# First expert layer: every token through every expert, or kept experts' tokens placed in 160 rows each

## The chip, the cores and the metric

The kernel runs on one core of one Trainium2 chip. The metric is the device time of one execution in microseconds (us). Three executions of the kernel before took 3815.05, 3818.07 and 3828.3 us; the median is 3818.07 us. Differences below about 0.3% (11.5 us) can't be told from no change here.

## What is computed

The program is a chain of layers over x, 16 sequences of 64 tokens with 256 features: T = 1024 tokens, held as 8 tiles of 128 tokens. Before the part that changes stands a linear-attention encoder of four layers (`l0_attn`), after it a slot attention over a context of 1601 rows for each sequence (`l1_xattn`). The part itself is a mixture of experts; x is layer-normed on the way in and the result is added to x:

```
logits = x @ gate_w.T;  probs = softmax(logits)
top2_w, top2_idx = top_k(probs, 2)
cap = int(1.25 * T / E)                       # 160 for T = 1024, E = 8
counts = bincount(top2_idx.reshape(-1), length=E);  keep = counts <= cap
comb[t, e] = top2_w where e is one of t's two experts, times keep[e]
h = relu(einsum('th,ehf->tef', x, W1) + b1);  y = einsum('teh,ehf->tef', h, W2) + b2
out = einsum('te,tef->tf', comb, y)
```

So an expert chosen more than 160 times gives nothing at all, and a kept expert has at most 160 tokens.

## The kernel before

Everything is in float32. A product in float32 shows as two records on the matrix engine (PE), so "x16" of a product is 8 of them.

**`l0_attn` (L408 to L735)** runs the encoder in two halves of 512 tokens, `a` and `b`. Its order is written by hand: generators (`project`, `attend`, `feed`) yield after each piece of PE work and `go(it, n)` (L650) advances one of them n pieces. While `self.pinned` is set, the engines keep the order of the program for PE (`mm`, `tr`), VectorE (`V`), ScalarE (`A`) and GpSimd (`G`). The last calls are `go(fd)` (rest of `feed(a)`), `go(feed(b, w, True))` and `squares(999)` (L732 to L734). `feed` (L613) turns the normed tokens, evacuates one half on VectorE and one on ScalarE (`turn`, L461), makes 8 products of 512 columns for the hidden layer (`by_feature`), then 4 tiles of tokens from them (`by_token`), norms the result and, in the last layer, adds it to x (`finish`, L642).

Between these pieces ScalarE squares the context for the next stage: `context_squares` (L242) has 16 x 13 = 208 squares of 128x256, loaded three pieces ahead; `squares(n)` advances it by n. A `feed` asks for 1 or 2 after each hidden product and for 4, 4, 4, 2 after the tiles of tokens, 26 in all.

**`l0_ffn` (L752 to L794)** norms all of x (`layernorm`), turns it (`transpose`) into xT, makes the logits tile by tile (`lin`), then on VectorE and ScalarE softmax, ranks and selection, counts each expert's tokens by a product with ones (L775), and makes `comb`. The experts' second bias is added as comb times b2 (L785). Then `weighted_experts` (L737) takes the 8 experts one after the other: 8 products of 512 columns into hT (`lin_t`, L180), relu alternating between VectorE and ScalarE (`bias_relu`), 16 products of 256 columns (`lin`, L193), and for every tile x += comb[:, e] * product (L746). All 1024 tokens go through all experts. PE, VectorE and ScalarE are ordered here by the framework's scheduler.

Each expert's two weights (256 KB each) go into a ring of 8 buffers (`w2`, L103), so four experts' weights are there at most. SyncE (SP) issues the loads in the order that the scheduler gives it; an issue that waits holds those behind it.

**`l1_xattn` (L796)** begins with two context loads for the first slot tile (`load_keys`, `cT`, 1664 KB each), whose buffers lie over memory that `l0_ffn` used, so that they wait for the tile they overlap (here xT, last read by `lin_t`). Its first scores need x of the first tile and both `cT`.

Of the kernel before, what the change touches and what calls it, by code (L numbers as in the profile page):

```python
# [11 lines left out]
F32 = mybir.dt.float32  # L12
I32 = mybir.dt.int32
# [50 lines left out]
class Sections:  # L64
# [343 lines left out]
    def l0_attn(self):  # L408
        nc, tc, d = self.nc, self.tc, self.d
        HT = NT // 2  # L410
        with ExitStack() as ctx:
# [260 lines left out]

            less = sb.tile([P, 1], F32, tag="minus", name="minus")
# [59 lines left out]
            go(feed(b, w, True))  # L733
            squares(999)  # L734
            self.pinned = False  # L735
# [16 lines left out]
    def l0_ffn(self):  # L752
        nc, tc, d = self.nc, self.tc, self.d
        E = 8
        with ExitStack() as ctx:
            sb = ctx.enter_context(tc.tile_pool(name="l0f", bufs=1, reuse_waits="tile"))
            sb2 = ctx.enter_context(tc.tile_pool(name="l0f2", bufs=2, reuse_waits="tile"))
            ps = ctx.enter_context(tc.tile_pool(name="l0f_ps", bufs=2, space=PSUM, reuse_waits="tile"))
            wg = sb.tile([P, KC, E], F32, tag="wg", name="wg")
            nc.sync.dma_start(wg, d["L0_ffn_gate_w"].rearrange("(c p) n -> p c n", p=P))  # L760
            b2 = sb.tile([E, D], F32, tag="b2", name="b2")
            nc.sync.dma_start(b2, d["L0_ffn_b2"])
            xln = sb.tile([P, NT, D], F32, tag="xln", name="xln")
            xT = sb.tile([P, KC, T], F32, tag="xT", name="xT")
            self.layernorm(sb, self.x, xln)
            self.transpose(ps, xln, xT)
            probs = sb.tile([P, NT, E], F32, tag="probs", name="probs")
            self.lin(ps, wg, xT, lambda t, pm: self.copy(probs[:, t, :], pm))
            self.softmax_small(sb, probs, E)
            sel = self.ranks(sb, probs, E)  # L770
            nc.vector.tensor_scalar(sel, sel, 1.5, None, ALU.is_lt)
            cnt = sb.tile([P, E], F32, tag="cnt", name="cnt")
            nc.vector.tensor_reduce(cnt, sel.rearrange("p t e -> p e t"), AX.X, ALU.add)
            pc = ps.tile([P, E], F32, tag="mm", name="pc", padded_shape=[P, 512])
            nc.tensor.matmul(pc, self.c("ones"), cnt, start=True, stop=True)  # L775
            keep = sb.tile([P, E], F32, tag="keep", name="keep")
            cap = int(1.25 * T / E)
            nc.vector.tensor_scalar(keep, pc, float(cap), None, ALU.is_le)
            comb = sb.tile([P, NT, E], F32, tag="comb", name="comb")
            nc.vector.tensor_tensor(comb, probs, sel, ALU.mult)  # L780
# [1667 lines left out]
def _consts():  # L2448
# [20 lines left out]
        "odd": (np.arange(P)[:, None] % 2 == np.arange(2)[None, :]).astype(np.float32),  # L2469
    }  # L2470


def _buckets():

    rp = np.maximum(np.arange(S)[:, None] - np.arange(S)[None, :], 0)
# [109 lines left out]
```

## Time and profile before

| what | value |
| --- | --- |
| median of three runs | 3818.07 us |
| the profiled execution | 3822.79 us |
| its span | 3821.0 us |
| granted PE clock, mean | 0.964 |
| PE, VectorE, ScalarE, GpSimd busy | 92%, 52%, 38%, 33% of the span |
| last `feed` and `l0_ffn` | about 1286 to 1464 us of the span |

The profiled execution is one of its own, 1.8 us longer than its span and 4.7 us longer than the median. The profile is read in four ways here: the chain of work that ended last (start, duration, engine, tile, line, number of records), a table of busy time by stretches (busy us and number of instructions for each engine, granted PE clock, share of DMA time, GB/s), the instructions of one engine in order of time (start, duration, line, operation; in brackets how long the engine was idle before and what released it), and the list of DMA queues. Lines of the pinned helpers show as L2233 (products), L2238 (transposes) and L58 (VectorE, ScalarE, GpSimd in `l0_attn`).

### The profile page before, as it was taken

To read this page: it belongs to the slowest core of one execution; us is meant where nothing else is said; L and a number is where in the kernel's file an instruction comes from. 1 tells how busy PE (TensorE), PEld (TensorE's weight loads), DVE (VectorE), ACT (ScalarE), POOL (GpSimd) and SP (SyncE) were. 2 spreads that over 40 slices of the span, in tenths; PEclk is the share of its full clock that TensorE was granted. 3 is DMA by queue.
4 is the path that set the end of the run, shared out by engine and by line. 5 is a ranking of instruction groups with operands and counts; after the bars stand their busy time and mean duration, and the time that the engine had idled before them with its cause. 6 is when DMAs were issued, how large, how long until landed. Compare 5 with 4: busy or idle time off the path is not lost.

```text
span 3821.0 us, 71159 instructions
## 1 busy us (share of the span) xinstructions
PE 3522.3 (92%) x31163; PEld 2225.8 (58%) x31178; DVE 1991.1 (52%) x3664; ACT 1457.4 (38%) x2080; POOL 1260.9 (33%) x755
## 2 busy tenths in 40 slices
PE   8999999996999899999987898999999879999986
PEld 4555555563666555555545566676767655555454
DVE  4333333335555546566556644577776655333346
ACT  3333333333444302444433433366666612111214
POOL 1555555551110002334331100477777630000012
PEclk9999999998999899999989999999999979999997
DMA  3111110001333214422301000311111004111650
GB/s 124 37 37 37 37 37 22 35 27 46 100 98 95 78 31 171 144 99 81 108 25 40 1 6 0 110 37 55 38 55 37 8 4 168 36 42 32 249 201 13
DMA packets 99678, 248.86 MB, mean 65 GB/s; under 512 B 8180, under 2 KB 69247, under 8 KB 97192
## 3 DMA queue, kind: packets, MB, share of 16 engines
q1 hardware_dynamic: 92456, 217.05, 16.0%
q10 hardware_dynamic: 6912, 27.27, 2.3%
q8 instruction: 245, 4.01, 0.4%
q14 instruction: 65, 0.53, 0.0%
HBM read 243.24 MB, written 1.05 MB: 64 GB/s over the span
## 4 chain that ended last, share of the span: by engine, by line
PE 77%; DVE 12%; ACT 8%; issue 2%; POOL 1%; DMA 0%; ACTq 0%; DVEq 0%; SPq 0%; POOLq 0%
PE sc L2233 15%; PE pk L2233 14%; PE lin L2233 7%; PE acc L2233 6%; PE lin_t L2233 5%; PE lin L193 5%; ACT e L321 4%; PE pu L2233 4%; PE gate L1798 3%; PE up L1798 3%; PE pc L1420 3%; PE prz L2233 2%; PE lin_t L180 2%; PE gelu_t L1330 2%; PE turn L2238 2%
## 5 line engine op out<-in xcount | busy, mean ns | idle before, releaser
L2166 POOL TENSOR_TENSOR tot<-tot,e 128x1024 f32<-128x1024 f32 (+1 forms) x340 | 803.5, 2363 | 373.8 <-ACT e L321 250.9
L264 DVE TENSOR_REDUCE m<-sc 128x4 f32<-128x2048 f32 x96 | 220.1, 2293 | 270.6 <-PE sc L2233 269.6
L1560 DVE SCALAR_TENSOR_TENSOR e<-sc,row_L_xattn_nbias,free 128x2048 f32<-128x2048 f32 x104 | 244.3, 2349 | 122.2 <-PE sc L2233 118.3
L1562 ACT ACTIVATE e<-e 128x2048 f32<-128x2048 f32 x104 | 198.7, 1911 | 243.2 <-DVE e L1560 243.2
L321 ACT ACTIVATE e<-sc 128x2048 f32<-128x2048 f32 x104 | 195.2, 1877 | 241.1 <-PE sc L2233 231.9
L2233 PE MATMUL sc<-qb,kT 32*128 32x128 f32 x6656 | 245.0, 283 | 36.5 <-DVE m L278 12.3
L2233 PEld LDWEIGHTS sc<-qb,kT 32*128 32x128 f32 x6656 | 206.1, 187 | 80.6 <-issue 24.5
L2233 PE MATMUL acc<-e,v 128*32 128x128 f32 x6656 | 226.3, 276 | 6.4 <-ACT e L1563 6.4
L2233 PEld LDWEIGHTS acc<-e,v 128*32 128x32 f32 x6656 | 170.0, 110 | 105.8 <-issue 95.2
L2233 PE MATMUL pk<-cT,wk 128*128 128x512 f32 (+1 forms) x512 | 206.4, 532 | 3.6 <-DVE rows L294 3.6
L2233 PE MATMUL pk<-wv,cT 128*128 128x256 f32 x832 | 208.6, 392 | 0.0
L1563 ACT ACTIVATE e<-e 128x2048 f32<-128x2048 f32 x104 | 198.7, 1911 | 3.3
L2233 PE MATMUL pk<-cT,wkv 128*128 128x512 f32 (+1 forms) x512 | 196.4, 524 | 0.0
L965 POOL TENSOR_TENSOR e<-e,mx 128x512 f32<-128x512 f32 x96 | 81.7, 883 | 347.1 <-DVE mx L964 347.1
L2233 PE MATMUL pk<-wkv,cT 128*128 128x256 f32 x832 | 196.3, 386 | 0.0
L2233 PEld LDWEIGHTS pk<-wv,cT 128*128 128x128 f32 x832 | 149.2, 189 | 75.3 <-issue 57.2
L2233 PEld LDWEIGHTS pk<-wkv,cT 128*128 128x128 f32 x832 | 153.2, 190 | 28.5 <-issue 4.3
L1420 PE MATMUL pc<-ew,eh 128*128 128x256 f32 x640 | 155.4, 385 | 0.0
L2233 PE MATMUL sc<-kT,qb 32*128 32x512 f32 (+2 forms) x1536 | 140.5, 465 | 13.3 <-issue 1.7
L1802 ACT ACTIVATE g<-gate 128x512 f32<-128x512 f32 x68 | 40.6, 597 | 292.2 <-PE gate L1798 292.2
L2233 PE MATMUL pu<-cn,e 128*64 128x257 f32 (+1 forms) x1248 | 142.7, 385 | 5.6 <-POOL e L975 5.6
L1803 DVE TENSOR_TENSOR hT<-up,g 128x512 f32<-128x512 f32 x68 | 47.0, 692 | 178.7 <-PE up L1798 174.6
(489 smaller groups left out, 6456.5 us busy)
## 6 DMA issues: line engine op xcount, KB each, us to landing
cT<-in_ctx_t SPq DMA_DIRECT2D x128, 832.0 KB
cn<-in_ctx_n SPq DMA_DIRECT2D x32, 1664.0 KB
piece<-in_ctx_n ACTq DMA_DIRECT2D x32, 640.0 KB
w<-in_L_attn_W SPq DMA_DIRECT2D x8, 1024.0 KB
piece<-in_ctx_n ACTq DMA_DIRECT2D x16, 384.0 KB
w<-in_L_ffn_W SPq DMA_DIRECT2D x16, 256.0 KB
down<-in_L_ffn_w_down SPq DMA_DIRECT2D x16, 256.0 KB
gate<-in_L_ffn_w_gate SPq DMA_DIRECT2D x16, 256.0 KB
```

Source lines behind the costliest of these rows:

```text
L180: nc.tensor.matmul(pm, w[:, k, n * P : (n + 1) * P], xT[:, k, h * 512 : (h + 1) * 512], start=(k == 0), stop=(k == kc - 1),)
L193: nc.tensor.matmul(pm, xT[:, k, t * P : (t + 1) * P], w[:, k, :], start=(k == 0), stop=(k == kc - 1))
L264: nc.vector.tensor_reduce(x.m4[:, g, :, i], pm, AX.X, ALU.max)
L321: nc.scalar.activation(e, pm, AF.Exp, scale=0.25)
L965: pin(nc.gpsimd.tensor_tensor(p.e, p.e, p.mx.unsqueeze(2).to_broadcast(p.shape), ALU.subtract))
L1420: nc.tensor.matmul(pc[:, n, j, :], s.eh[i][:, c, tok], ew2[:, c, cols], start=False, stop=(c == 3))
L1560: nc.vector.scalar_tensor_tensor(e16, pm16, nb, free[:, at : at + P].unsqueeze(1).to_broadcast([P, 16, P]), ALU.add, ALU.mult)
L1562: nc.scalar.activation(e, e, AF.Relu)
L1563: nc.scalar.activation(e, e, AF.Square)
L1798: nc.tensor.matmul(pm[-1], w[:, k, n * P : (n + 1) * P], xT[:, k, tok], start=(k == 0), stop=(k == KC - 1))
L2166: nc.gpsimd.tensor_tensor(tot[:w], x.first if c == 1 else tot[:w], e[:w], ALU.add)
L2233: ins = self.nc.tensor.matmul(*args, **kw)
```

## The change

Routing moves into `l0_attn`. A new generator `route(s)` norms one half of x, turns it, makes the half's logits, ranks the experts for each token, counts with products against a strict upper triangle (`prior`) and ones how many tokens before this one chose each expert, and so gives each of a token's two choices a place: expert times 160 plus that count, or a spare row of its own where the count is 160 or more. Eight indirect DMAs for each half, issued by GpSimd, write the normed tokens by these places to `taken` in DRAM (1280 rows and 2048 spare ones, the 1280 set to zero beforehand by one DMA from SP). `route(a)` is interleaved with `feed(b)`, `route(b)` comes after it, and `squares(999)` stands ahead of that `feed(b)` where it stood behind it.

`l0_ffn` reads `taken` back: for each expert its first 128 rows into `xs`, and the last 32 rows of the eight experts, four to a tile, into `xw`. It turns them into xsT (160 columns for each expert), makes softmax and the weights `wt` of the two choices, and runs each expert on its own 160 rows: 4 products of 160 columns, relu, 2 products of 256 columns for the first 128 rows; after four experts their last 32 rows go together, in four strips of one tile. The second bias is added on the way out. Results go to `given` in DRAM by SP; 16 indirect DMAs on GpSimd fetch them by token (`got`), and two steps per tile on VectorE add them to x with their weights. The weights' ring is as before. A constant array `places` is loaded, and `b2` of the experts becomes a row of `rows`.

The diff, cut; of `l0_ffn` only lines of the new body are shown, the old one stands above.

```diff
+        self.routed = ExitStack()
+        pool = self.routed.enter_context(tc.tile_pool(name="l0r", bufs=1, reuse_waits="tile"))
+        self.route = to = Streamed(0)
...
+        wg = pool.tile([P, KC, E], F32, tag="wg", name="wg")
+        nc.sync.dma_start(wg, d["L0_ffn_gate_w"].rearrange("(c p) n -> p c n", p=P))
+        places = pool.tile([P, d["places"].shape[1]], F32, tag="places", name="places")
...
+        self.taken = tc.dram_tile([E * CAP + 2 * T, D], F32, name="taken")
+        self.given = tc.dram_tile([E * CAP, D], F32, name="given")
+        zero = pool.tile([P, D], F32, tag="zero", name="zero")
+        nc.gpsimd.memset(zero, 0.0)
+        nc.sync.dma_start(
+            self.taken[: E * CAP].rearrange("(j p) d -> p j d", p=P), zero.unsqueeze(1).to_broadcast([P, E * CAP // P, D]))
+        views = dram_disjoint_views(self.taken, 2 * NT)
...
+            def route(s):
+                i = slice(s.i * HT, (s.i + 1) * HT)
+                for p in range(2):
+                    measure(s, s.x, p)
+                for p in range(2):
+                    norm(s, s.x, p)
+                yield
+                for p in range(2):
+                    turn(s, p)
+                    yield
+                pm = ps.tile([P, HT, E], F32, tag="mm", name="gate", bufs=3, padded_shape=[P, 64, E])
+                for t in range(HT):
+                    for k in range(KC):
+                        self.mm(pm[:, t, :], s.hT[:, k, t * P : (t + 1) * P], wg[:, k, :], start=(t == 0 and k == 0),
+                                stop=(k == KC - 1), skip_group_check=True)
+                own = to.logits[:, i]
...
+                V.tensor_tensor(gt, other, each, ALU.is_gt)
+                V.tensor_tensor(eq, other, each, ALU.is_equal)
+                V.tensor_tensor(eq, eq, low, ALU.mult)
+                V.tensor_tensor(gt, gt, eq, ALU.add)
+                rank = sb.tile([P, HT, E], F32, tag="rank", name="rank", bufs=2)
+                V.tensor_reduce(rank, gt, AX.X, ALU.add)
+                sel = sb.tile([P, HT, E], F32, tag="sel", name="sel", bufs=2)
+                V.tensor_scalar(sel, rank, 1.5, 0.0, ALU.is_lt, ALU.add)
+                yield
...
+                self.mm(pos, prior, sel, start=True, stop=False, skip_group_check=True)
+                for t in range(HT - 1):
+                    n = HT - 1 - t
+                    self.mm(pos[:, t + 1 :, :], self.c("ones"), sel[:, t : t + 1, :].to_broadcast([P, n, E]), start=False,
+                            stop=(s.i == 0), skip_group_check=True)
+                if s.i:
+                    self.mm(pos, self.c("ones"), to.count[:, 0:1, :].to_broadcast([P, HT, E]), start=False, stop=True,
+                            skip_group_check=True)
+                V.tensor_reduce(to.count[:, s.i], sel.rearrange("p t e -> p e t"), AX.X, ALU.add)
...
+                place = sb.tile(shape, F32, tag="place", name="place", bufs=2)
+                many = pos.unsqueeze(2).to_broadcast(shape)
+                V.tensor_tensor(place, many, at, ALU.add)
+                fits = sb.tile([P, HT, E], F32, tag="fits", name="fits", bufs=2)
+                V.tensor_scalar(fits, pos, CAP - 0.5, 0.0, ALU.is_lt, ALU.add)
+                V.tensor_tensor(to.hot[:, i], to.hot[:, i], fits.unsqueeze(2).to_broadcast(shape), ALU.mult)
+                V.tensor_tensor(place, place, to.hot[:, i], ALU.mult)
+                one = sb.tile([P, HT, 2], F32, tag="one", name="one", bufs=2)
+                V.tensor_reduce(one, place, AX.X, ALU.add)
+                V.tensor_tensor(one, one, spare[:, i], ALU.add)
+                V.tensor_copy(to.put[:, i], one)
+                V.tensor_scalar(to.get[:, i], one, E * CAP - 1.0, 0.0, ALU.min, ALU.add)
+                for t in range(HT):
+                    for k in range(2):
+                        j = 2 * (s.i * HT + t) + k
+                        nc.gpsimd.indirect_dma_start(
+                            views[j], bass.IndirectOffsetOnAxis(ap=to.put[:, s.i * HT + t, k : k + 1], axis=0),
+                            s.n[:, t, :], None)
+                yield
...
             go(fd)
-            go(feed(b, w, True))
             squares(999)
+            fd, rt = feed(b, w, True), route(a)
+            go(fd, 4)
+            go(rt, 1)
+            go(fd, 2)
+            for _ in range(4):
+                go(rt, 1)
+                go(fd, 1)
+            go(fd)
+            go(route(b))
             self.pinned = False
...
+            xs = sb.tile([P, E, D], F32, tag="xs", name="xs")
+            xw = sb.tile([P, 2, D], F32, tag="xw", name="xw")
+            ys = sb.tile([P, E, D], F32, tag="ys", name="ys")
+            yw = sb.tile([P, 2, D], F32, tag="yw", name="yw")
+            xsT = sb.tile([P, KC, E, CAP], F32, tag="xsT", name="xsT")
+            got = sb.tile([P, NT, 2, D], F32, tag="got", name="got")
...
+            for e in range(0, E, 2):
+                nc.sync.dma_start(xs[:, e : e + 2], taken[:P, e : e + 2])
+            for r in range(4):
+                nc.sync.dma_start(xw[W * r : W * (r + 1)], last(taken, r))
...
+            hs = []
+            for e in range(E):
+                w1, w2 = self.w2(d["L0_ffn_W1"][e], "w1"), self.w2(d["L0_ffn_W2"][e], "w2")
+                pm = ps.tile([P, KC, CAP], F32, tag="mm", name="hidden", padded_shape=[P, KC, 256])
+                for n in range(KC):
+                    for k in range(KC):
+                        nc.tensor.matmul(pm[:, n, :], w1[:, k, n * P : (n + 1) * P], xsT[:, k, e, :],
+                                         start=(n == 0 and k == 0), stop=(k == KC - 1), skip_group_check=True)
+                hT = sb.tile([P, KC, CAP], F32, tag="hT", name="hT", bufs=6)
+                for n in range(KC):
+                    self.bias_relu(hT[:, n], pm[:, n], b1[:, 2 * e + n : 2 * e + n + 1])
+                po = ps.tile([P, D], F32, tag="out", name="out", padded_shape=[P, 512])
+                for k in range(KC):
+                    nc.tensor.matmul(po, hT[:, k, :P], w2[:, k, :], start=(k == 0), stop=(k == KC - 1))
+                nc.vector.tensor_tensor(ys[:, e], po, b2[:, e * D : (e + 1) * D], ALU.add)
+                nc.sync.dma_start(given[:P, e], ys[:, e])
+                hs.append((hT, w2))
+                if e % 4 == 3:
+                    q = e // 4
+                    po = ps.tile([P, D], F32, tag="out", name="out", padded_shape=[P, 512])
+                    for k in range(KC):
+                        for r, (hT, w2) in enumerate(hs):
+                            nc.tensor.matmul(po[W * r : W * (r + 1), :], hT[:, k, P:], w2[:, k, :], start=(k == 0),
+                                             stop=(k == KC - 1))
+                    nc.vector.tensor_tensor(yw[:, q], po, b2w[:, q], ALU.add)
+                    for r in range(4):
+                        nc.sync.dma_start(given[P:, 4 * q + r], yw[W * r : W * (r + 1), q])
+                    hs = []
             for t in range(NT):
+                for k in range(2):
+                    nc.gpsimd.indirect_dma_start(
+                        got[:, t, k, :], None, self.given, bass.IndirectOffsetOnAxis(ap=to.get[:, t, k : k + 1], axis=0))
+                for k in range(2):
+                    nc.vector.scalar_tensor_tensor(
+                        self.x[:, t, :], got[:, t, k, :], wt[:, t, k : k + 1], self.x[:, t, :], ALU.mult, ALU.add)
+        self.routed.close()
```

## The prediction

> **What bounds the kernel now.** The page's first block comes first: PE is busy 92% of the span, VectorE 52%, ScalarE 38%, GpSimd 33%. A mean over eleven stages says little about this one, so the chain of waits for 1230 to 1500 us comes next.
>
> ```profile
> 1286.11 15.92 PE lin_t L2233 x32
> 1302.02 10.38 PE lin L2233 x48
> ...
> 1344.45 7.26 PE pb L785 x16
> 1351.71 8.64 PE lin_t L180 x16
> 1360.35 6.91 PE lin L193 x32
> 1367.26 6.87 PE lin_t L180 x16
> ...
> 1456.77 6.92 PE lin L193 x32
> 1463.71 0.48 DVE x L746
> ...
> 1469.77 5.81 PE sc L2233 x32
> ```
>
> Columns: start, duration, engine, tile, line, records. The expert loop is PE from 1351.71 to 1463.7, 112.0 us with no other engine between, 6.9 + 6.9 us per expert; the next stage's first scores start at 1469.77. The stretches say the same:
>
> ```profile
> 1286.00:1316.00 30.00, 29.73 (x96) 18.96 (x96) 8.62 (x25) 14.35 (x59) 0.00 (x0) 0.93 0.30 97
> 1316.00:1325.00 9.00, 2.10 (x8) 1.14 (x8) 8.73 (x37) 0.97 (x5) 2.92 (x3) 0.76 0.00 1
> 1325.00:1352.00 27.00, 18.78 (x67) 14.51 (x68) 13.66 (x39) 4.70 (x13) 0.47 (x3) 0.50 0.00 0
> 1352.00:1464.00 112.00, 112.00 (x387) 70.73 (x387) 42.93 (x81) 12.29 (x17) 0.00 (x0) 0.99 0.15 46
> ```
>
> Busy us of PE, weight loads, VectorE, ScalarE, GpSimd; then PE clock, DMA share, GB/s. `feed(b)` (first row) is bound by PE, so is the expert loop; the 36 us between are latency, at a halved clock. ScalarE's order in time shows what stands ahead of `feed(b)`:
>
> ```profile
> 1282.52 0.20 ACT L58 ACTIVATE ln_r<-ln_r 128x2 f32<-128x2 f32 x1 [3.65 <-DVE ln_r L58]
> 1285.64 1.02 ACT L58 ACTIVATE hT<-tr,vecs 128x256 f32<-128x256 f32 x2 [2.91 <-DVE hT L58]
> ```
>
> Between `feed(a)`'s last root and `feed(b)`'s hT ScalarE is idle. The DMA queues show which kind of DMA the kernel has:
>
> ```profile
> q1 hardware_dynamic: 92456, 217.05, 16.0%
> q10 hardware_dynamic: 6912, 27.27, 2.3%
> ```
>
> These are SP's and ScalarE's loads. No row is a DMA issued by GpSimd, so none prices the 32 that come in.
>
> **The change, part by part.** I measure from the last `y` addition of `feed(b)` (1315.99) to the first scores (1469.77): 153.8 us before.
>
> *squares(999) ahead of feed(b).* Each `feed` asks for 12 + 14 = 26 squares; eight take all 208. Behind the last `feed` the call emits none, ahead of it 26. ScalarE's order is pinned, so they stand between the two rows above. A square takes 0.40 us from start to start (1290.51, 1290.91), a piece load costs an idle 0.41: 26 x 0.40 + 4 x 0.41 = 12.0, from 1282.6 to 1294.6. Behind them wait the two hT evacuations (1.02), and behind these all of `feed(b)`'s PE work: 1295.6 instead of 1286.66, 9 us; pieces that come late (3.3 MB in 12 us) make it 10. Bounds: 0 if the squares could run under earlier waits, but the root at 1282.52 is ahead of them; 13 if every piece is waited for. That ScalarE is then free during `feed(b)` gains nothing: PE is busy 29.73 of 30 there. Cost 10.
>
> *route(a) inside feed(b).* PE is the bound, so its products add: 8 transposes at 0.11 (four in 0.44 at 1262.12) 0.9; 8 logit products at 0.44 (24 records, 12 products, in 5.31 at 1328.92) 3.5; 5 counting products at 0.44, 2.2. Waits: the transposes behind norms (VectorE some 5 us, two pieces of cover at 1.7 each) 1.3, the counting behind the ranks 0.7. Cost 8.6 (6 to 12). Its VectorE work (15 us at most, VectorE is busy 8.6 of 30) is hidden, and so are its 8 indirect DMAs on GpSimd, idle there: 14 us of `by_token` cover them; uncovered they would cost what b's cost. The 1.3 MB of zeros, `wg` and `places` lie under `l0_attn`'s 450 us; SP's in-order queue could hold the weights behind the zeros only until GpSimd's memset at the stage's start. Zero, at worst 2.
>
> *Out: the old front and loop.* The 153.8 us go. In, one after the other:
>
> 1. x of b done after the last addition: stats, root, norm, scale, add, 4.1 (by the rows from 1278 to 1285).
> 2. `route(b)`, now pinned behind: two `measure` pairs 2 x 1.36, roots and norms 1.9, transposes and copy 1.9, the rest of the logits 3.2, ranks on half the width 2.3 (3.7 for the whole, 1337.33 to 1341.06), counting 2.3, seven small steps of VectorE at 0.25: 16.1.
> 3. 8 indirect writes, and their landing.
> 4. The load of `xs` and `xw`, 1.3 MB: a 256 KB load takes 2.2 us from issue (1360.38) to last byte (1362.6), bursts run at 300 GB/s (821 to 826): 6.2, and the last transposes and copies 1.5: 7.7.
> 5. The expert loop. A product of 160 columns lies between 128 (1.17 for four, 0.29 each, at 1468.09) and 512 (0.86): 0.34, four 1.35; two of 256 at 0.432, 0.86; the strips of four experts 0.86 if they run side by side as `acc`'s do (32 records, 16 products, in 1.01), twice. Sum 8 x 2.21 + 1.7 = 19.4. Relu hand-offs of 0.6 if each expert waits for its own: 4.8; the slow start 1.8 (8.64 against 6.87); the weights of experts 4 to 7, which sit with the stores in SP's queue, 2: 28.
> 6. Last stores: 4 issues and landing, 3.6.
> 7. 16 indirect reads, landing, last addition.
> 8. The next stage. `got` is 16 KB in a stage that grows from 43 to 65 KB per partition; by the order of allocation a `cT` buffer of the first slot tile lies on it, so its 1.66 MB start after the last addition: 1.2 + 1.66/0.39 = 5.5, with issue and receipt 6.2 until scores (6.1 before). Queries are ready by then.
>
> *The price of an indirect DMA* decides. Nearest rows: an SP issue takes 0.38 us, and its 256 KB land in 2.2. The Trainium skill's page "DMA: Bandwidth & Descriptors" (Anatomy of one DMA — SWDGE) gives each DMA from GpSimd about 2.0 us fixed plus bytes at 436 GB/s, 2.3 us for these 128 KB; its table of latencies puts the fixed part mostly into the receipt, which doesn't hold the next issue, and the start into about 1 us of emission. By the row alone, 24 exposed ones cost 9 us; by the rule, one after the other, 55 us, a rule that speaks against this change. I take emission 1.0 plus an issue 0.33 = 1.3 each (an estimate), and 2.0 landing once for each group: writes 8 x 1.3 + 2.0 = 12.4, reads 16 x 1.3 + 2.0 + 1.0 = 23.8. Bounds 0.4 to 2.3; each 0.1 is 2.4 us. No run here shows it yet.
>
> Sum: 4.1 + 16.1 + 12.4 + 7.7 + 28 + 3.6 + 23.8 + 6.2 = 101.9. Saved 51.9, less 10 + 8.6 = 33.3. Against the execution's own 3822.8: 3789.5; the median of the runs shown stands 4.7 lower: 3785.
>
> *The clock* is a second place for a rule. The row 1325 to 1352 has PE busy 18.78 of 27 us and still only 0.50 granted; at 1351.7 the loop needed some 3.4 us to leave it. The skill's page "TensorE: Matmul & The Clock Gate" (Part 1) says half rate after an idle window of 3.4 us, full after a busy one: by the rule a loop of 20 us warms up and costs 1.8; by the row, if hand-offs keep it broken up like that stretch, it stays halved: 2 x 19.4 + 7 = 46 instead of 28. I take the rule, since products of 160 and 256 columns are denser than those with 8 in that row.
>
> **Rivals.**
>
> *Cheap DMAs.* GpSimd emits one in 0.7 us: 24 x 0.6 = 14 less, 3771. For it: nothing else runs on GpSimd. [...]
>
> *The loop waits.* Stores and weights in one SP queue: w1 and w2 of experts 5 to 7 are issued only when the store ahead of them goes, 3 us each time, and the clock stays half for most: 28 becomes 45, 3802. For it: SP's order before already waits on PE for each load. Against: the scheduler moved loads ahead there.
>
> *Slower.* GpSimd takes 3.2 us for each indirect DMA, as it would if fetching the 128 offsets, one from each partition, cost more than writing the descriptors: 24 x 1.9 = 46 more, 3830, 12 slower than before. It decides from 2.7 us (33.3/24 above 1.3). For it: no row bounds it. Against: it exceeds the page's whole time for such a DMA.
>
> *The change does not do what it says*: PE's work shrinks, but the stage keeps its length because everything is serial latency. That is the case of both last rivals together; the list above has only 19 of 102 us on PE.
>
> **How the numbers follow.** The forecast (indirect DMA 1.0 to 1.7 us, loop 24 to 34 us: 3773 to 3797) has 0.48; cheap DMAs 0.20; the loop waits 0.18; within 0.3% of before 0.08; slower 0.06 beyond that bound. 0.3% is about what a measurement of this kernel can tell from no change: 3806.6 to 3829.5 counts as same. Part of the waiting case falls into it (0.03). So faster 0.83, same 0.11, slower 0.06. Eight in ten: 3764 to 3812, which leaves 0.07 below (cheap DMAs and a loop at 22 us) and 0.12 above.
>
> **What would show it.** ScalarE: 26 squares in a row after 1282.6, and the first hidden product of `feed(b)` near 1296; if it stays at 1286, step one is wrong. GpSimd: 8 issues after `route(b)`, 16 after the last store, 1.3 us apart; the distance is the price. PE in the loop: busy about 20 to 26 of 28 us, clock back to 1.0 after the first experts; at 0.5 the waiting rival holds. SP: the second `cT` issued right after the last addition. The forecast is wrong if the indirect DMAs cost over 2 us, or if x of the first tile is held back further than these lists say.

## The result and the profile after

The changed kernel took 3792.44 us (median of 4, 3786.28 to 3794.34) beside 3819.35 us for the kernel before in the same runs: a ratio of 0.9924, 95% interval 0.9902 to 0.9945. A second comparison of the same two kernels gave 0.9909 (0.9893 to 0.9926; 3788.21 against 3825.11 us). The medians gained 26.9 and 36.9 us, both beyond the 0.3% that can't be told from no change. The forecast, 33.3 us off 3818, was a ratio of 0.9913. The profiled execution took 3790.97 us with a span of 3789.2, 31.8 under the span of before.

The chain of waits of the changed kernel, from 1240 to 1470 us (start, duration, engine, tile, line, records), against the two feed-forward rows and the loop shown of before:

```profile
1285.15 2.11 ACT junk L59 x10
...
1298.14 5.12 PE lin_t L2387 x6
...
1332.98 0.42 DVE y L59
...
1352.83 1.03 POOL taken L758
...
1364.31 0.38 SPq L880
1365.76 5.18 DMA xs<-taken
...
1374.10 3.90 PE hidden L919 x14
...
1388.79 3.02 DMA w<-in_L_ffn_W
...
1402.21 0.97 POOL got L943
...
1421.19 4.43 DMA got<-given,get
1425.71 0.48 DVE x L946
...
1432.22 7.83 PE sc L2387 x31
```

The path is what the prediction laid out, in its order: squares, `feed(b)` with `route(a)` in it, `route(b)`, writes, loads, loop, fetches, next stage. No new wait of another kind stands in it. The first scores start at 1432.22 instead of 1469.77, 37.6 us sooner. The same stretches by engine (busy us of PE, weight loads, VectorE, ScalarE, GpSimd; then PE clock, DMA share, GB/s):

```profile
1286.00:1298.00 12.00, 2.07 (x2) 0.50 (x2) 2.21 (x4) 10.77 (x51) 0.00 (x0) 0.50 0.55 173
1298.00:1333.00 35.00, 33.38 (x126) 21.98 (x126) 15.81 (x51) 4.40 (x10) 7.93 (x8) 0.93 0.26 90
...
1374.00:1398.00 24.00, 21.86 (x135) 18.20 (x136) 7.94 (x23) 4.43 (x9) 0.00 (x0) 0.92 0.58 170
1398.00:1432.00 34.00, 3.50 (x14) 2.38 (x12) 12.75 (x43) 2.06 (x11) 17.82 (x21) 0.55 0.67 212
```

The first row is ScalarE almost alone, squaring (each square shows as two instructions). The third is the expert loop: 24 us in place of 112, PE busy for nine tenths of them and warm. The last is the price of moving rows: PE almost idle for 34 us while GpSimd issues. Its order in time shows that price (start, duration, form, and in brackets the idle time before it and what ended it):

```profile
1402.19 0.99 POOL L943 DMA_INDIRECT got<-given,get  x1 [38.51 <-DMA wo<-in_L_attn_w_o]
1403.48 0.96 POOL L943 DMA_INDIRECT got<-given,get  x1 [0.30 <-issue]
```

0.96 us busy and 0.30 between: about 1.26 from start to start (1.29 the first time, 1.25 for most of the later ones). The load of `wo` that the first line names is not what the fetches need; it landed at about that time: in the second profile of this kernel the chain goes from the last store to `given`, which the fetches read, to the first fetch. The queue's row on the page, absent before, is `q0 software_dynamic: 1536, 4.20, 0.4%`. 0.4% of the span is 14 us of the sixteen DMA engines' time for all 32 indirect DMAs, 0.43 each: a third of what GpSimd spends on one.

### The profile page after: what moved, and what is told of

The parts are those of the page before. It is cut to its first block, busy times and chain, and to the rows that moved or that the text cites. A ratio compares the mean times of both kernels' runs of the same rounds, so it can differ in the third digit from the quotient of the medians.

```text
span 3789.2 us, 70696 instructions
## 1 busy us (share of the span) xinstructions
PE 3440.1 (91%) x30923; PEld 2179.8 (58%) x30938; DVE 1965.6 (52%) x3634; ACT 1450.4 (38%) x2072; POOL 1290.4 (34%) x788
## 3 DMA queue, kind: packets, MB, share of 16 engines
q0 software_dynamic: 1536, 4.20, 0.4%
## 4 chain that ended last, share of the span: by engine, by line
PE 76%; DVE 12%; ACT 8%; issue 2%; POOL 1%; DMA 1%; SPq 0%; ACTq 0%; DVEq 0%; POOLq 0%
PE sc L2387 15%; PE pk L2387 15%; PE lin L2387 7%; PE acc L2387 6%; PE lin_t L2387 5%; ACT e L322 4%; PE pu L2387 4%; PE lin L194 3%; PE gate L1952 3%; PE up L1952 3%; PE pc L1574 3%; PE prz L2387 2%; PE gelu_t L1484 2%; PE turn L2392 2%; PE pn L2387 1%
## 5 line engine op out<-in xcount | busy, mean ns | idle before, releaser
L2387 PE MATMUL sc<-cT,qT 128*64 128x512 f32 (+1 forms) x768 | 141.5, 521 | 0.5 <-DVE qT L1077 0.5
```

Of the source, the lines that this page charges most:

```text
L2387: ins = self.nc.tensor.matmul(*args, **kw)
```

## The experiments

My theory was the prediction's: the stretch is one chain of steps, each at the price of its own rows, and GpSimd's issue is the price of an indirect DMA. The rivals were that the data or the landing is that price, that the next stage waits for its context loads, and that what the stretch gains is lost again further on. Each kernel below is the changed kernel with one edit, or with several where it says so. "Landmark" is the time from `feed(a)`'s last root on ScalarE (before: 1282.52, changed: 1284.71) to the first product of weights and context rows, `pu` (before: 1491.0, changed: 1454.3): 208.5 us before, 169.6 and 169.7 in two profiles of the changed kernel. It leaves out what other stages do, but not the clock: from the first scores to `pu` the changed kernel takes 22.1 us in both of its profiles, and 24.3 to 24.4 in four of the others (squares behind, rows laid elsewhere, scratch elsewhere, more instructions). In each of these four the eight `pw` products just ahead of `pu` ran at a granted clock near 0.5 and took 5.4 to 5.5 us, where the changed kernel's first profile has 2.85. About 2.2 us of a landmark is therefore a matter of the clock.

| kernel | median us | ratio to before | landmark us |
|---|---|---|---|
| changed, two comparisons | 3792.44, 3788.21 | 0.9924, 0.9909 | 169.6, 169.7 |
| squares behind | 3778.64 | 0.9869 (0.9844 to 0.9893) | 164.5 |
| fetches twice | 3805.44 (one run) | | 187.5 |
| fetches of half the rows | 3795.37 (one run) | | 167.9 |
| fetched rows laid elsewhere | 3789.44 | 0.9905 (0.9883 to 0.9927) | 172.7 |
| additions by tile | 3782.91 | 0.9885 (0.9864 to 0.9906) | 162.9 |
| tables later | 3789.56 | 0.99 (0.9877 to 0.9922) | 169.5 |
| tables later, scratch elsewhere | 3789.03 | 0.9912 (0.9896 to 0.9929) | 169.2 |
| three together | 3773.98 | 0.9867 (0.9849 to 0.9885) | 153.1 |
| late additions | 3764.36 | 0.9855 (0.9835 to 0.9875) | 143.9 |
| more instructions | 3789.7 | 0.9909 (0.9894 to 0.9923) | 172.9 |

**The squares.** `squares(999)` goes behind `feed(b)` again:

```
-            squares(999)
             fd, rt = feed(b, w, True), route(a)
...
             go(fd)
+            squares(999)
             go(route(b))
```

> The 26 context squares stand behind feed(b) again; all else as in the changed kernel. Theory (the stretch is one chain, and the squares head it): hT and the first hidden product of feed(b) come 9.8 us earlier and so does everything behind, since ScalarE idles 11.8 us inside the last linear product; 9.8 us under the changed kernel, about 3782.6, ratio to before 0.9904. Rival (the squares were covered by other waits, and the time goes to the next wait: route(a) then stands behind the norms with less cover, or the squares only move ahead of route(b)'s roots on ScalarE): under 3 us.

From its chain of waits:

```profile
1287.06 0.92 DVE hT L59 x2
1288.02 5.65 PE lin_t L2387 x8
...
1321.10 0.42 DVE y L59
...
1343.51 1.03 POOL taken L758
```

In the changed kernel PE makes one product of `feed(b)` at 1288.30 and then waits until 1298.14 for the half of hT that ScalarE evacuates; here it goes on at once. By the seventh product the lead is 9.6 us (1295.64 instead of 1305.23), and 9.3 of it still stand at the first write (1343.51 instead of 1352.83). So the squares were on the path. Two parts are given back: the loop meets longer waits for weights (2.73 and 3.85 us instead of one of 3.02), so that the first scores are 7.8 earlier, and the landmark is only 5.1 shorter, because this is one of the four profiles with the slower `pw` products (5.49 us). The theory holds for the place; of its 9.8 us about half arrive at the landmark. The median is 9.6 and 13.8 us under the two of the changed kernel, and 10.8 under two others measured beside it that differ little from the changed one (rows laid elsewhere, tables later); its interval allows both the whole and the half, and the profiled execution, at 3784.66, was the slowest of its four.

**The price of a fetch.** Every fetch is issued twice:

```
+            got2 = sb.tile([P, 2, D], F32, tag="got2", name="got2")
...
+                    for o in (got2[:, k, :], got[:, t, k, :]):
-                    nc.gpsimd.indirect_dma_start(
-                        got[:, t, k, :], None, self.given, ...)
+                        nc.gpsimd.indirect_dma_start(o, None, self.given, ...)
```

> Each of the 16 fetches is issued twice, the first time into a spare tile. Theory (GpSimd's issue is the price, 1.26 us from start to start, the landing lies under the next issue): 16 x 1.26 = 20.2 us more between the first fetch and the last addition (24.0 becomes 44.2), first scores at 1452.4. Rival (the price is the landing of the last fetch and the queue's start, shared by all): under 5 us more. Second rival (the data of the DMA engines is the limit: 2 MB more at some 360 GB/s): about 6 us more.

The scheduler set 5 of the 16 spare fetches behind the last one that is needed, so 11 stood in front: 11 x 1.26 = 13.9 was to be expected of the issue, and the first scores came at 1445.5, 13.3 later. The start of the fetches was the same (1402.14). The data rival, 1.4 MB at 360 GB/s, would be 4 us. The price is by issue; the expected 20.2 was too much because I hadn't foreseen the order.

Then the same 16 instructions with half the rows each:

```
-                        got[:, t, k, :], None, self.given, ...(ap=to.get[:, t, k : k + 1], axis=0))
+                        got[:64, t, k, :], None, self.given, ...(ap=to.get[:64, t, k : k + 1], axis=0))
```

> Each fetch brings the rows of partitions 0 to 63 only; the other half of every tile of fetched rows is zero from a clearing ahead of the loop, so half of the tokens go without their experts. Theory A (the price of a fetch is by instruction): 1.26 us from start to start as before, 24.0 us becomes 22 to 23.5 with an earlier last landing. Theory B (it is by row, one descriptor each): 0.63 to 0.8 us from start to start, 24.0 becomes 14 to 16.

GpSimd's order in time:

```profile
1404.19 0.91 POOL L944 DMA_INDIRECT got<-given,get  x1 [0.30 <-issue]
1405.40 0.90 POOL L944 DMA_INDIRECT got<-given,get  x1 [0.30 <-issue]
1406.60 0.90 POOL L944 DMA_INDIRECT got<-given,get  x1 [0.30 <-issue]
```

1.20 from start to start instead of 1.25, and 22.0 us from the first fetch to the end of the last addition instead of 24.0: theory A. If the price is a fixed part and one by row, 64 rows cost 0.05 us and the fixed part is 1.15, an estimate from these two sizes. Fewer DMAs with more rows each, or shorter rows, were not tried.

**The next stage's start.** Prediction step 8 said that a context buffer lies on the fetched rows, so that its load waits for the last addition. Here they share no bytes:

```
             xs = sb.tile([P, E, D], F32, tag="xs", name="xs")
+            got = sb.tile([P, NT, 2, D], F32, tag="got", name="got")
             xw = sb.tile([P, 2, D], F32, tag="xw", name="xw")
...
-            got = sb.tile([P, NT, 2, D], F32, tag="got", name="got")
```

> The tile of the fetched rows is laid between xs and xw, so that it shares no bytes with the first two context buffers of the next stage. Theory (the chain ends in VectorE: last addition, layer norm, queries): the first scores move by nothing, and only the first piece's 7.8 us shrink to the 5.8 of before: 0 to 2 us under the changed kernel, 3790.4 to 3792.4. Rival (the context loads that start only after the last addition are the wait): 6 us or more, 3786.

```profile
1403.75 3.03 SPq L972 DMA_DIRECT2D cT<-in_ctx_t  x4
1433.30 7.71 PE L2387 MATMUL sc<-cT,qT 128*64 128x512 f32 x32 [0.52 <-DVE qT L1077]
1452.19 5.49 PE L2387 MATMUL pw<-wih,wv 128*128 128x512 f32 x8 [3.71 <-DVE mvg L1035]
```

All four parts of the first two context buffers were issued by 1406.8, but the first scores came at 1433.3 (changed: 1432.2), and their first piece still took 7.4 us from its first product to its last. The loads were not the wait, and the long piece is not theirs either: its slowest records take nearly twice those of the same form (1116 ns against 592), and the clock granted from 1433 to 1437 was 0.50. The prediction had named the wrong cause for a term whose size was right. The landmark grew by 3.1, most of it after the scores: the `pw` products of the third line wait as long as in the changed kernel (3.72 us there) but take 5.49 us for 2.85, at a clock of 0.53 from 1452 to 1458.

VectorE is the cause: it adds all eight tiles before it norms the first. So the fetches go into the next stage, into buffers of its context rows, and each tile is added by itself:

```
+            for t in range(NT):
+                for k in range(2):
+                    nc.gpsimd.indirect_dma_start(got[t][:, k, :], None, self.given, ...)
...
             product(mqk, wq, wk, w_s)
+            add(0)
             first(tiles[0])
...
+            add(1)
             keys(b[0])
+            for t in range(2, NT):
+                add(t)
```

> The 16 fetches stand in the next stage, each tile's addition by itself: the first token tile is added, normed and asked for its queries before the other seven are added; the fetched rows lie in buffers of the context rows. Theory (24 us of fetches are on the path only because VectorE adds all eight tiles before the first norm): the first scores need 2 of 16 fetches: 1402.2 + 2 x 1.26 + landing 2 to 4.4 + addition 1 + norm and queries 6 = 1414 to 1416 instead of 1432.2, and the first tile's scaling on VectorE behind all additions at 1427 instead of 1441; 12 to 18 us under the changed kernel, 3774 to 3780, ratio 0.989 or less. Rival (the context buffers' loads are what the next stage waits for, or its products catch up with the later tiles): under 5 us.

The first scores start at 1417.0, 15.2 earlier, near the theory; the first context product comes only 6.7 earlier by the landmark, near the rival. The stretches show why (as above; DMA share and GB/s are the last two):

```profile
1404.00:1410.00 6.00, 0.00 (x0) 0.00 (x0) 0.25 (x1) 0.00 (x0) 4.67 (x5) 0.50 0.98 353
1410.00:1417.00 7.00, 2.76 (x10) 2.07 (x10) 2.84 (x11) 1.19 (x5) 5.29 (x6) 0.50 1.02 391
1417.00:1424.00 7.00, 5.52 (x16) 2.31 (x16) 6.52 (x19) 0.92 (x4) 5.78 (x7) 0.77 1.08 313
1424.00:1432.00 8.00, 3.62 (x26) 2.06 (x26) 3.99 (x8) 1.37 (x2) 0.74 (x2) 0.91 0.95 236
```

The DMA engines are full from 1404 on, with the context loads that now run under the fetches. The last fetch, issued at 1421.65, takes 9.98 us to land instead of 4.43; its addition ends at 1432.2, and the first tile's scaling stands behind it on VectorE, at 1436.76. A wait removed has become a transfer that is contended: both accounts were half right.

**The start of the attention stage** lost 2.2 us where the prediction had "zero, at worst 2". First only the order in SP's queue was changed:

```
-        nc.sync.dma_start(wg, ...); nc.sync.dma_start(places, d["places"]); ...
...
             w = weights(0)
+            nc.sync.dma_start(wg, ...); nc.sync.dma_start(places, d["places"]); ...
```

> In the attention stage the gate's weights, the table of places, and the zeros with their clearing are issued behind the first layer's weights. Theory: the row for the keys lands 2.2 us sooner again, as before the change, and all behind it: 2.2 us less, 3790.2. Rival (another wait of the stage's start is as late): 0.

The row for the keys was still asked for only at 860.36, now ahead of `wg`. The time from the previous stage's last addition to the last root was 424.0 us (changed: 424.7 and 423.8 in two profiles; before: 422.5 and 422.7). The addresses explain the late issue: `route`'s scratch of 3.4 KB lies at the end of the stage's space, moves everything else down by as much, and the row comes to lie on a buffer that the previous stage reads until 860. So the scratch got a pool at the other end as well:

```
+            scratch = ctx.enter_context(tc.tile_pool(name="l0s", bufs=1, reuse_waits="tile"))
...
-                gt = sb.tile(shape, F32, tag="rk_gt", name="rk_gt")
+                gt = scratch.tile(shape, F32, tag="rk_gt", name="rk_gt")
...
```

> Gate weights, places and zeros behind the first weights, and the scratch of route() in a pool at the other end, so that the row for the keys has its address of before and is asked for at 822 instead of 862. Theory (the start lost 2.2 us by that row): the attention stage from its first addition to its last root is as long as before, 2 us shorter than the changed kernel; 3790. Rival (the loss is scatter of the previous stage's end and of the clock): within 0.7 us of the changed kernel's, and 3792.

The row is asked for at 822.38 and the 9.41 us for which GpSimd waited for it are gone, but the stage is 423.7 us long: at most 1 us is won. Matched instruction by instruction on VectorE, the rest comes in one or two steps of about 1 us, at places that differ from profile to profile, and there PE's clock is lower. In the changed kernel's first profile the step lies between 898 and 907 us; before, and changed:

```profile
895.00:905.00 10.00, 7.89 (x15) 3.27 (x15) 5.01 (x10) 1.94 (x4) 0.55 (x1) 0.71 0.00 0
```

```profile
895.00:905.00 10.00, 8.31 (x13) 3.41 (x12) 4.60 (x10) 1.79 (x3) 0.39 (x1) 0.50 0.00 0
```

In its second profile, and in this kernel, the step lies at the first feed-forward products near 937, with 0.66 granted from 930 to 940 where before had 0.83: those eight products take 6.61 us here and 5.27 before. The kernel with the squares behind, whose row is as late as the changed kernel's, met neither and lost 0.3 (422.9 us). So of the 2.2 us at most 1 is the row, and the rest goes with the clock. The traces show a window: in all fourteen profiles each record of the granted clock lasts a whole multiple of 3.41 us, and the grid of its changes lies between 0.02 and 3.19 us behind the start of the span. The Trainium skill's page "TensorE: Matmul & The Clock Gate" (Part 1) says that the window by which the clock is granted runs freely, so that the same products meet it in another phase from run to run; that fits these records.

**Together.** Squares behind, tables and scratch moved, additions by tile:

> Squares behind feed(b); gate weights, places and zeros behind the first weights, and the scratch of route() in a pool of its own at the other end, so that the stage's buffers lie where they lay before; additions by tile in the next stage. Theory: the three are on one chain one after the other and add up: first scores 7.8 earlier by the squares, 15.2 by the additions, 2.2 by the start: 1407; the first context product (1454.3) follows by 7.8 + 6.4 + 2.2 = 16.4; time 16 us under the changed kernel, 3776. Rival (the context loads at the head of the next stage take all of the DMA engines, so the squares' part is kept only because these move too, and the start's part is lost to another wait as it was when the tables alone were moved): 10 to 13 us.

First scores at 1408.5 and first context product at 1437.55, 16.8 us earlier: near the 1407 and the 16.4 of the theory, but not by its parts. The start, outside the landmark, gave 0.3 instead of 2.2, and the landmark became 16.5 shorter where the squares and the additions should have given 14.2 of it. The time, 3773.98, follows; its four executions lie between 3763.89 and 3780.41.

Then the additions of tiles 2 to 7 go behind the first tile's weights:

```
-            for t in range(2, NT):
-                add(t)
-            load_rows(tiles[1])
             biases()
             attend(tiles[0], tiles[1])
...
+            for t in range(2, NT):
+                add(t)
+            load_rows(tiles[1])
```

> As the three together, but the additions of tiles 2 to 7, and the context rows of tile 1 that take their buffer, stand behind the first tile's weights. Theory (the first tile's scaling waited on VectorE behind additions whose rows landed late, under the context loads): the scaling comes with its scores, the first context product 5 to 8 us before that of the three together, time 3769 to 3772. Rival (the first context product waits for the context rows' load, which is as late): within 2 us of the three together.

The first tile's scaling on VectorE, in the three together and here:

```profile
1426.46 0.67 DVE L1120 TENSOR_TENSOR e<-turn,rr 128x512 f32<-128x512 f32 x1
```

```profile
1416.61 0.69 DVE L1120 TENSOR_TENSOR e<-turn,rr 128x512 f32<-128x512 f32 x1
```

With the scores at 1408.5 and 1409.0 it comes 9.9 us sooner, so it did wait behind the additions. The landmark is 9.2 us shorter again (5 to 8 were expected). The time, 3764.36, is the best here: ratio 0.9855, a gain of 1.45% where the change itself has 0.76 and 0.91%. Against the three together the traces decide; the two intervals overlap.

**What the later stages took back.** In the first pair of profiles the first context product was 36.7 us earlier, the end only 31.8. To see whether that is scatter, both kernels were profiled again:

> The kernel before, unchanged, profiled once more. Theory (the 5 us between what the stretch gained and what the time gained are scatter of the later stages, which all kernels share): last context product to the end 1851 to 1862 us as in the ten profiles so far; the stretch itself again within 1 us (first scores less the last feed-forward addition 153.8). Rival (the change slows a later stage): before stays at 1851 and all kernels with the change lie above it.

> The changed kernel, unchanged, profiled once more. Theory: stretch 116.3 us within 1.5, time 3786 to 3795; the start of the attention stage 1 to 2.5 us behind that of the kernel before. Rival (as beside the other): a tail of 1855 us or more again while before's stays at 1851.

From the last context product to the end, the kernel before took 1851.3 and 1850.2 us, the changed one 1855.5 and 1852.0. That alone decides little. Matched instruction by instruction on VectorE, though, the self-attention that follows was slower in every one of the eleven profiles with the change up to here, by 1.9 to 4.1 us against the first profile of before and 2.4 to 4.5 against the second, while its instructions and their order were the same as before. The first slip has one place. PE's order in time, before:

```profile
2035.98 0.45 PE L2233 MATMUL sc<-kT,qb 32*128 32x64 f32 x8
2038.17 0.90 PE L2233 MATMUL sc<-kT,qb 32*128 32x64 f32 x24 [1.74 <-issue]
```

and changed, with PE's clock just behind it:

```profile
1998.77 0.85 PE L2387 MATMUL acc<-eT,ones 64*32 64x64 f32 x58
2001.60 0.31 PE L2387 MATMUL acc<-eT,ones 64*32 64x64 f32 x6 [1.97 <-issue]
```

```profile
2004.00:2009.00 5.00, 4.93 (x151) 4.25 (x152) 2.77 (x3) 2.23 (x3) 0.00 (x0) 0.50 0.00 0
```

"issue" means that the engine waited for nothing that the profile shows. Before, the stall falls into a set of scores, and the clock behind it stays at 1.00 (2040 to 2050). In the changed kernel it falls 58 records into a row sum of 64: the clock is 0.50 for 5 us behind it, and VectorE's reciprocal, which the chain needs, waits 2.25 us longer than it did before. The reciprocal before, and changed:

```profile
2035.03 1.76 DVE L2381 RECIPROCAL rec<-acc 128x256 f32<-128x256 f32 x1 [2.80 <-PE acc L2233]
```

```profile
2001.96 1.76 DVE L2535 RECIPROCAL rec<-acc 128x256 f32<-128x256 f32 x1 [5.05 <-PE acc L2387]
```

The second profile of the changed kernel has the stall at the same instruction (1.88 us). Counted from the start of PE's stream, with four instructions for a float32 product (two weight loads, two products), both places have the same remainder when divided by 256. The last experiment moves the boundary: 55 products of 8 columns, 220 instructions, in the time in which PE waits for the fetched rows anyway:

```
             product(mqk, wq, wk, w_s)
+            idle = ps.tile([P, 512], F32, tag="sc", name="idle", bufs=2)
+            for i in range(55):
+                self.mm(idle[:, :8], self.c("ones"), self.ident[:, :8], start=(i == 0), stop=(i == 54))
             first(tiles[0])
```

> The changed kernel with 55 more products of 8 columns, which nobody reads, behind the product of Wq and Wk, in the 24 us in which PE waits for the fetched rows. They lengthen PE's stream by 220 instructions (two weight loads and two products each). Theory (PE stalls 1.5 to 2 us once in the self-attention at a boundary of 256 instructions of its stream: in the kernel before, that place is ahead of the ninth record of the scores, in the changed one ahead of the last six of a row-sum; counted so, both have the same remainder by 256): the stall moves back to the ninth record of the scores; the clock of 0.50 behind it goes, and the self-attention takes the 2 to 4 us less that it took before the change; last context product to the end 1850 to 1853, time 3785 to 3788. Rival (the stall belongs to a load that is under way then, or to the clock): it stays ahead of the last six of the row-sum, and nothing moves but the first scores' piece, 7.8 to 5.8 us, on a PE that is warm.

```profile
2004.16 0.45 PE L2390 MATMUL sc<-kT,qb 32*128 32x64 f32 x8
2006.36 0.90 PE L2390 MATMUL sc<-kT,qb 32*128 32x64 f32 x24 [1.75 <-issue]
```

The stall is back ahead of the ninth record of the scores, the self-attention is within 0.5 us of the kernel before, and the last context product to the end takes 1850.0 us. The theory holds for the place. The time did not fall (3789.7): the profiled execution lost 2 us ahead of the stretch and 3.3 in the landmark, of which 2.2 are the slower `pw` products again; the expected 3785 to 3788 was missed. So what the stall costs the whole kernel is not shown. In five of the eleven profiles that have it in the row sum less than 1 us of the loss is left some 350 us further on (in the two of the changed kernel 0.5 and 4.3), and by the end the same instructions lie between 1.3 us ahead of before and 10.8 behind.

What PE waits for can be read from the DMA queue that carries instructions, before, changed, and with 220 more:

```profile
q8 instruction: 245, 4.01, 0.4%
```

```profile
q8 instruction: 243, 3.98, 0.4%
```

```profile
q8 instruction: 244, 4.00, 0.4%
```

Each packet has 16 KB, and there is one for every 256 of PE's instructions (62682, 62206 and 62441 records, waiting ones included). In the changed kernel PE worked off the 256 instructions ahead of the stall in 2.7 us, from 1996.90. The packet for the next block started at 1999.19 and took 1.00 us, and PE went on at 2001.60, 1.4 behind it. All fourteen profiles say the same of every place where PE idles for more than 0.7 us and "issue" ends it: in each profile these places lie multiples of 256 records apart (within two), the block ahead was done in 2.7 to 4.1 us, and PE goes on 1.2 to 1.7 us after the packet has landed. So the stall is a fetch of instructions that comes too late behind a block that is worked off quickly.

The Trainium skill's page "Runtime: NRT & Kernel Launch" (Instruction fetch mechanics) says that an engine's instructions are fetched in blocks of 256 and that crossing a boundary is mostly hidden. The block agrees with these runs; the hiding doesn't here: 1.5 to 2.5 us at this boundary and, in all but one profile, 0.7 to 1.5 at another some 20 us later.

The rival of a load under way is half answered. At the first of the two places the DMA engines are busy with loads of the stage behind (a share of 0.85 from 1996.9 to 1999.2), yet the packet was no slower than most (median 1.04). At the second they are idle (0.02 from 2016.3 to 2018.7), and the packet starts as late, 2.3 us behind its boundary. So no load is needed for such a stall; whether the loads delay the first packet, and why the second is late, is open.

## Why the prediction was right

| step | predicted us | measured us |
|---|---|---|
| start of the attention stage | 0, at worst 2 | 2.2 |
| squares ahead of `feed(b)` | 10 | 9.8 |
| `route(a)` in `feed(b)` | 8.6 | 5.0 |
| x of b, `route(b)` | 20.2 | 19.8 |
| 8 writes and landing | 12.4 | 11.5 |
| loads of `xs`, `xw`, transposes | 7.7 | 9.8 |
| expert loop | 28 | 23.3 |
| last stores | 3.6 | 4.8 |
| 16 fetches, landing, addition | 23.8 | 24.0 |
| to the first scores | 6.2 | 6.0 |

From the last addition of `feed(b)` to the first scores: 101.9 predicted, 99.2 measured. Net: 153.8 - 99.2 - 9.8 - 5.0 - 2.2 = 37.6 saved at the first scores, against 33.3. The spans fell by 31.8 and 33.7, closer to the forecast than that, and this is in part luck: the stretch gained 4.3 us more than forecast, and later stages, of which the forecast had nothing, lost 5.8 in the first pair. Within the sum, too, terms that were too dear (the loop, `route(a)`) and too cheap (the loads, the stores, the start) offset each other.

- **The squares** were right in size and mechanism: 26 of them between two rows of ScalarE's pinned order. Moving them back brought the seventh product of `feed(b)` 9.6 sooner. (The 9.8 of the table runs to 1298.14. Counted at the seventh product it is 9.3, and `route(a)` has the other 0.5.)
- **The price of an indirect DMA**, which the prediction called decisive, was 1.26 against an estimate of 1.3. By the 2.0 us plus bytes that the Trainium skill's page "DMA: Bandwidth & Descriptors" (Anatomy of one DMA — SWDGE) has for each, the 16 fetches would have taken 37 us one after the other (an estimate); they took 24.0 with the landing, so the fixed part does not hold the next issue. The landing was 2.4 us for the last write and 4.4 for the last fetch, instead of 2.0. The rival of 3.2 us for each, which ends slower than before, is refuted by GpSimd's rows, as is the cheap one of 0.7.
- **`route(a)`** was 3.6 us too dear. Half of that is its 16 gate records, priced from a stretch at half clock (3.5 us); inside `feed(b)` the clock is 0.93 and they took 1.70. Another 1.1 is its counting, priced as five products (2.2) where there are four, which took 1.06.
- **The loads** were 2.1 too cheap. They were priced at 300 GB/s from 821 to 826; that stretch moved 199 GB/s in the mean, and 1364 to 1371, the loads' own, 187. SP alone needed 3.8 us for their eight issues.
- **The loop** was 4.7 too dear: most of the eight hand-offs of 0.6 don't occur, because PE runs the next expert's hidden products before the output of this one. The rivals of the halved clock and of waits in SP's queue came down to a slow start (3.90 for the first hidden products, 2.00 where the scratch lies elsewhere) and one wait for weights (3.02).
- **The next stage's start** was right in size (6.0 for 6.2) for a wrong reason. The load of the overlapped context buffer did not set it; VectorE's last addition, norm and queries did, as the kernel with the rows elsewhere shows.
- **The start** failed as a step at "zero": the order of SP's queue was weighed, but not that new scratch shifts every buffer below it. That cost at most 1 us; the rest goes with the clock.
- **What was missing**: a cost in a stage that the change does not touch. Removing instructions moved a boundary of PE's stream to a place on the chain: 4.1 and 3.1 us in the two profiles at the self-attention (against the first profile of before), of which the second regained most later. In the first pair of profiles it is most of what lies between the 36.7 us at the first context product and the 31.8 of the spans. The second pair, 3820.1 and 3786.4, differ by 33.7.

## What to carry to other kernels

Price GpSimd's indirect DMAs by the instruction, count those that nothing covers, and ask what the first consumer needs: here 2 of 16 fetches were enough to start the next stage, and adding by tile, late, with the squares moved, was worth nearly as much again as the change. Before hiding a wait under transfers, look at the DMA share of the stretch it moves into. When a large change gains less than its stretch did, match the untouched stages instruction by instruction: a loss may sit where nothing was edited, and may be made good again further on.

## What the runs showed of the hardware

- An indirect DMA of 128 rows of 1 KB holds GpSimd for 0.96 us and 0.30 more until the next; with 64 rows 0.90 and 0.30. So nearly all of it is by the instruction.
- The last of 16 such fetches landed 4.4 us after its issue, and 10 us after it where the DMA engines were full (share 0.95 to 1.08).
- PE's instructions come in packets of 16 KB, one for 256 of them. Where a block of 256 was worked off in 2.7 to 3.0 us, PE stalled 1.5 to 2.5 us until 1.2 to 1.7 us after the next packet had landed, and the stall moved with the boundary when 220 instructions were added.
- The granted clock changed only on a grid of 3.41 us, which lay differently to the start in each profile. The same eight products took 5.27 or 6.61 us, by the clock granted in that stretch (0.83 or 0.66), in kernels with the same instructions in that place.
